# Attention of a two-layer trunk: instructions in a fixed order, weights folded in pieces with vector-engine transposes, and the values' bias as a weighted sum

## The chip, the cores and the metric

The kernel runs on one core of one Trainium2 chip. The metric is the device time of one execution in microseconds; the kernel before takes 2160.85 us, the median of three runs (2158.11 to 2163.81). All data are 32-bit floats.

## The reference

Two layers, each `x + attention(norm(x)) + ffn(norm(x))`, on x of shape (4, 512, 512).

- Layer 0's attention is a recurrence over 32 steps of 16 tokens ("TTT"): per head a small weight matrix is updated by a gradient step; the output is normalized and projected. Its feed-forward part is a gated one of width 1408.
- Layer 1's feed-forward part has four experts; every fourth token goes to the same one.
- Layer 1's attention is what the change is mainly about. Per batch, with 16 heads of 128:

```
c_kv = x @ W_DKV + b_DKV                 # 128 wide
k = c_kv @ W_UK + b_UK;  v = c_kv @ W_UV + b_UV
c_q = x @ W_DQ + b_DQ                    # 384 wide
q = c_q @ W_UQ + b_UQ
q[:, :64] = rope(q @ W_QR);  k[:, :64] = rope(k @ W_KR)   # 32 rotated, 32 zeros
out = softmax(q k^T / sqrt(128)) v @ W_O + b_O
```

## The kernel before, in words

The work lies in three stages, one after the other.

**The recurrence** (L86 to L774) steps through 32 blocks. A step is a serial chain across TensorE (PE), VectorE (DVE), ScalarE (ACT) and GpSimd (POOL). Into its gaps the program puts other work: generators yield after each piece an estimate of its PE time in us, and `fill(us)` draws pieces until the budget is spent. `GAPS`, `LAST_GAPS` and `LAST_FINISH` (L37, L38) are the budgets: three per step, and those between the parts of the last `finish`. The filler is layer 0's feed-forward part (`gate_up`, `down`), projections of the next chunk, the finishing of the chunk before (`finish`), the latents c_kv and c_q of layer 1 (`latents`, L625 on, evicted by ACT at L637 into tiles with two buffers and stored in DRAM from ACT's queue), and `value_bias` (L522). The last works out what b_UV adds to the output: softmax rows sum to one, so it is the constant row b_UV @ W_O, which goes into `bo` beside b_O. For it each of four groups of heads loads four 128 x 512 tiles of W_O (wob), multiplies them on PE with b_UV spread over 32 columns, and adds the partial rows by a product with ones.

**The experts** (L801 to L921): for each of four, gate and up products (epg, epu; PSUM tags pg, pu), SiLU on ACT, a product on DVE, and the down product (epo), which DVE adds to y (L907); POOL then adds `bo` (L908). SP, the queue of SyncE, fetches weights ahead.

**Attention** (L928 on) works in units: 4 groups of heads (hg), 4 batches (b), 4 heads of the group (h), 64 units. Before a group its weights are folded (`group_weights`, L943), so that a unit needs fewer products:

- `turned` (L933): PE turns a 128 x 512 weight by four transposes against the identity (ptw), and ACT copies the result (wt).
- `fold`: four products with W_KR or W_QR (pw) replace the second half of the key or query columns with the columns that feed the rotation.
- For values, W_UV and W_O are multiplied into vo (pvo, L970), so v is never formed.

Group 0 is folded at the start of the stage; each next one when batch 1 of the group before begins. A unit is then:

- `queries_keys` (L987): one product for keys (pk), three for queries (pq); ACT evicts 64 rows with the bias, DVE multiplies with cosine and sine (`rotate`, t_k and t_q), POOL subtracts.
- `probabilities` (L1006), four times: a product of scores (sc, four PSUM buffers), DVE's maximum (mx), ACT's exponential with the sum (prob), DVE's reciprocal, ACT's scaling.
- `softmax` and `turn` (L1017, L1041): DVE transposes 32 x 32 blocks (tt), and 16 loads on SP's queue put the blocks in place (prT).
- `context` (L1051): four products with the latent (pc), copied by ACT into ctxT.
- After the last head of a batch, `project_out` (L1063): 16 products of ctxT and vo (po), four output tiles, which DVE adds to y.

The program records keys and queries of unit i, probabilities of unit i-1 and the context of unit i-3 in one turn of its loop. The order in which an engine gets them is a scheduler's, except where `tc.keep_in_program_order` is called: then instructions marked this way stay in the order in which they were recorded. Before the change only the tail and the experts' weight loads are marked. Tiles of a pool rotate over its buffers; an instruction that writes a buffer waits for the readers of its earlier contents.

Of the kernel before, what the change touches and what calls it, by code (L numbers as in the profile page):

```python
# [12 lines left out]
F32 = mybir.dt.float32  # L13
AF = mybir.ActivationFunctionType
ALU = mybir.AluOpType
# [21 lines left out]
GAPS, LAST_GAPS = (11.0, 4.0, 8.0), (10.0, 4.0, 5.0)  # L37
LAST_FINISH = (9.0, 17.0, 5.0)  # L38
# [17 lines left out]
def trunk_kernel(ctx: ExitStack, tc: tile.TileContext, a: dict, out: bass.AP):  # L56
# [32 lines left out]
    with ExitStack() as px:  # L89
# [424 lines left out]

        ones32 = one.tile([P, P], F32, tag="ones32", name="ones32")
        nc.vector.memset(ones32, 1.0 / 32)
        buv16 = one.tile([H, D], F32, tag="buv16", name="buv16")
        nc.gpsimd.dma_start(out=buv16, in_=a["b_UV"].rearrange("(h d) -> h d", d=D))
        buv_b = one.tile([P, H, 32], F32, tag="buv_b", name="buv_b")
        nc.gpsimd.dma_start(out=bo, in_=a["b_O"].unsqueeze(0).to_broadcast([P, HS]))  # L520

        def value_bias(hg):  # L522
            if hg == 0:
                pt = psum()[:, :H]
                nc.tensor.transpose(pt, buv16, ident[:H, :H])
                nc.vector.tensor_copy(buv_b, pt.unsqueeze(2).to_broadcast([P, H, 32]))
            pb = psum()
            for h, r in enumerate(quarters):
                w = wk.tile([P, HS], F32, tag="wd", name=f"wob_{hg}_{h}", bufs=4)
                nc.sync.dma_start(out=w, in_=a["W_O"][(4 * hg + h) * D : (4 * hg + h + 1) * D, :])  # L530
                mm(pb[r], buv_b[:, 4 * hg + h, :], w)
            part = wk.tile([P, HS], F32, tag="xt", name=f"bo_part{hg}", bufs=4)
            nc.vector.tensor_copy(part, pb)
            yield 1.3
            pb = psum()
            mm(pb, ones32, part)
            nc.vector.tensor_add(bo, pb, bo)
            yield 0.86

# [84 lines left out]
        def latents(key):  # L624
# [4 lines left out]
            for m, w in enumerate(lw):  # L629
# [6 lines left out]
                for b in range(B):  # L636
                    nc.scalar.activation(  # L637
                        to[:, b], view[:, :, b // 2, :, b % 2], AF.Identity, bias=lat_b[:, m : m + 1], scale=1.0
                    )
# [6 lines left out]
        nc.gpsimd.dma_start(out=lat_b[:, :1], in_=a["b_DKV"])  # L646
        nc.gpsimd.dma_start(out=lat_b[:, 1:], in_=a["b_DQ"])


        def between(ch):  # L650
# [12 lines left out]
            extra = value_bias(ch - 1) if 1 <= ch <= NHG else iter(())  # L663
# [13 lines left out]
            yield from extra  # L677
# [120 lines left out]
        for _ in chain(work, fin, latents(NCHUNK - 1)):  # L798
            pass
# [20 lines left out]

    with ExitStack() as px:
        one = px.enter_context(tc.tile_pool(name="d_one", bufs=1, reuse_waits="tile"))
        wk = px.enter_context(tc.tile_pool(name="d_wk", bufs=2, reuse_waits="tile"))
        wg = px.enter_context(tc.tile_pool(name="d_wg", bufs=1, reuse_waits="tile"))
        psp = px.enter_context(tc.tile_pool(name="d_ps", bufs=2, space=PSUM))
        gate_w = [one.tile([P, NC, 2 * EI], F32, tag="gu1", name="gu_1")]
# [11 lines left out]
        def downs(e):  # L838
            dn = wk.tile([P, EI // P, HS], F32, tag="dn", name=f"dn_{e}")
            fetch(out=dn, in_=a["dn"][e].rearrange("(c p) o -> p c o", p=P))  # L840
            return dn
# [27 lines left out]
        for e in range(E):  # L869
# [3 lines left out]
            if e == 1:  # L873
                nc.sync.dma_start(out=wqr, in_=a["W_QR"])
                nc.sync.dma_start(out=wkr, in_=a["W_KR"])
                nc.sync.dma_start(out=buk, in_=a["b_UK"])
# [10 lines left out]
            for i in range(EI // P):  # L887
                pg = psp.tile([P, B * P], F32, tag="pg", name=f"epg_{e}_{i}")
                product(e, pg, gu, i * P)
                pu = psp.tile([P, B * P], F32, tag="pu", name=f"epu_{e}_{i}")  # L890
# [6 lines left out]
            for b in range(B):  # L897
# [10 lines left out]
                nc.gpsimd.tensor_add(y[b][:, e, :], y[b][:, e, :], bo)  # L908
            if e == 1:

                for wr, bias in ((wkr, buk), (wqr, buq)):
                    pb = psp.tile([P, 512], F32, tag="pa", name="pb")
                    nc.tensor.matmul(pb[RD:, :H], lhsT=wr, rhs=bias, start=True, stop=True)
                    nc.vector.tensor_copy(bias[RD:, :], pb[RD:, :H])
                nc.vector.tensor_scalar_mul(buq[:RD, :], buq[:RD, :], scale)
# [12 lines left out]
    with ExitStack() as px:  # L928
# [4 lines left out]
        def turned(w, nm):  # L933

            pt = ps_pj.tile([P, HPG, P], F32, tag="pj", name=f"ptw_{nm}")
            for h in range(HPG):
                nc.tensor.transpose(pt[:, h, :], w[:, h, :], ident)
            t = wk.tile([P, HPG, P], F32, tag="wt", name=f"wt_{nm}")
            nc.scalar.copy(t, pt)
            return t  # L940

        def group_weights(hg):

            c = slice(hg * HPG * D, (hg + 1) * HPG * D)

            def loaded(name, src, bufs=2):
                t = wk.tile([P, HPG, src.shape[-1] // HPG], F32, tag=name, name=f"{name}_{hg}", bufs=bufs)
                nc.sync.dma_start(out=t, in_=src.rearrange("p (h d) -> p h d", h=HPG))
                return t

            def fold(w, wr, nm):
                wt = turned(w, f"{nm}_{hg}")
# [257 lines left out]
```

## Time and profile before

| | |
|---|---|
| median of three runs | 2160.85 us |
| the profiled execution | 2162.4 us |
| its span in the profile | 2160.6 us |
| recurrence, to the first expert product | 0 to 1022.4 us |
| experts | 1022.4 to 1191.9 us |
| attention | 1191.9 to 2160.6 us |

The profile shows one execution. Rows give the source line, the engine, the operation, the output and inputs by the program's names, the shape and a count. A 32-bit product shows as two records on PE. "PEclk" is the clock granted to TensorE as a share of full speed. An "SPq" row is SyncE issuing a DMA; its duration is the issue, not the transfer. A wait row says who waited for whom, with the total in us, the number of waits and the longest. After "|", group rows give busy time, the mean duration in ns, and the idle time just before.

### The profile page before, as it was taken

The numbers are of one execution on the slowest core, as the hardware profiler recorded it, in microseconds if no ns is written. First come the engines' busy times: TensorE is split into PE (matmuls) and PEld (weight loads), VectorE is DVE, ScalarE is ACT, GpSimd is POOL, SyncE is SP. The second block draws the span as 40 slices with busy tenths as digits, with TensorE's granted clock in tenths as the row PEclk, the third lists the DMA queues.
The fourth block names the chain that finished last, engine by engine and source line by source line (L and its number), as shares of the span: only waits on it lengthen the run. The fifth ranks groups of instructions, "written<-read, shape, count | busy, mean of one in ns | idle before, by whom it ended". The sixth has DMA issues, their size and how long they took to land.

```text
span 2160.6 us, 29279 instructions
## 1 busy us (share of the span) xinstructions
PE 2068.6 (96%) x10050; PEld 1181.5 (55%) x10050; DVE 1177.5 (54%) x2384; ACT 883.3 (41%) x1805; POOL 504.9 (23%) x555
## 2 busy tenths in 40 slices
PE   8999999999999999995999899999999999999998
PEld 6776676767676767543444444444444444444444
DVE  4445656465656565631111556664666656666663
ACT  2334353434434343332000454444544545455552
POOL 4233233233333333301001211110111111111110
PEclk9999999999999999998999989999999999999999
DMA  6556364646474646526610233333233333333332
GB/s 179 153 138 190 112 193 134 180 135 175 131 197 129 173 136 192 171 75 235 226 59 25 89 92 77 74 94 75 76 77 93 75 72 78 75 75 75 95 94 76
DMA packets 286960, 259.27 MB, mean 120 GB/s; under 512 B 52956, under 2 KB 210845, under 8 KB 285789
## 3 DMA queue, kind: packets, MB, share of 16 engines
q1 hardware_dynamic: 272752, 245.96, 41.0%
q10 hardware_dynamic: 11500, 5.32, 0.9%
q0 software_dynamic: 2560, 6.13, 0.8%
q8 instruction: 81, 1.33, 0.3%
q14 instruction: 67, 0.54, 0.1%
HBM read 161.60 MB, written 29.62 MB: 89 GB/s over the span
## 4 chain that ended last, share of the span: by engine, by line
PE 75%; DVE 10%; ACT 9%; DMA 3%; issue 2%; POOL 1%; SPq 0%; ACTq 0%; DVEq 0%; POOLq 0%
PE pj L100 14%; PE pf L100 11%; PE po L1069 10%; PE pc L1054 7%; PE sc L1008 5%; PE pq L999 5%; PE pd L100 5%; ACT prob L1013 3%; PE epg L855 3%; PE epo L900 3%; PE epu L855 3%; ACT prob L1015 2%; PE pso L100 2%; PE pk L992 2%; PE pz L100 2%
## 5 line engine op out<-in xcount | busy, mean ns | idle before, releaser
L1008 PE MATMUL sc<-kT,qT 96*128 96x512 f32 x512 | 235.7, 598 | 15.1 <-ACT prob L1013 13.5
L985 POOL TENSOR_TENSOR kT<-t_k,t_k 32x512 f32<-32x512 f32 x64 | 80.7, 1261 | 717.9 <-PE pq L999 403.3
L1013 ACT ACTIVATE prob<-sc,mx 128x512 f32<-128x512 f32 x256 | 173.1, 683 | 147.1 <-DVE mx L1010 147.1
L1069 PE MATMUL po<-vo,ctxT 128*128 128x512 f32 x512 | 223.0, 593 | 1.5 <-ACT ctxT L1059 1.5
L1054 PE MATMUL pc<-prT,lv 128*128 128x512 f32 x496 | 224.0, 594 | 0.0
L1023 DVE STREAM_TRANSPOSE tt<-prob 128x512 f32<-128x512 f32 x252 | 166.6, 697 | 60.3 <-ACT prob L1015 56.7
L100 PE MATMUL pf<-xT,wg 128*128 128x256 f32 x704 | 171.8, 385 | 4.2 <-DVE hid L459 3.9
L999 PE MATMUL pq<-cq,uq 128*128 128x512 f32 x384 | 175.2, 592 | 0.0
L1015 ACT ACTIVATE prob<-prob,sm 128x512 f32<-128x512 f32 x256 | 171.7, 724 | 3.6 <-DVE sm L1014 3.6
L1008 PEld LDWEIGHTS sc<-kT,qT 96*128 96x128 f32 x512 | 96.0, 191 | 140.9 <-issue 110.6
L100 PE MATMUL pf<-xT,wu 128*128 128x256 f32 x704 | 168.0, 380 | 0.5 <-DMA wu<-in_wu 0.3
L1010 DVE TENSOR_REDUCE mx<-sc 128x1 f32<-128x512 f32 x256 | 164.4, 681 | 7.0 <-PE sc L1008 4.4
L100 PE MATMUL pd<-wd,hid 128*128 128x512 f32 x352 | 165.2, 600 | 0.2
L1069 PEld LDWEIGHTS po<-vo,ctxT 128*128 128x128 f32 x512 | 97.1, 190 | 124.1 <-issue 116.2
L1054 PEld LDWEIGHTS pc<-prT,lv 128*128 128x128 f32 x496 | 94.5, 191 | 120.0 <-issue 112.1
L100 PEld LDWEIGHTS pf<-xT,wg 128*128 128x128 f32 x704 | 131.0, 190 | 32.1 <-DVE hid L459 6.7
L100 PEld LDWEIGHTS pf<-xT,wu 128*128 128x128 f32 x704 | 133.2, 190 | 22.1 <-issue 2.6
L1079 DVE TENSOR_TENSOR y<-po,y 128x512 f32<-128x512 f32 x64 | 44.2, 691 | 152.5 <-PE po L1069 152.5
L993 ACT ACTIVATE kT<-pk,b_UK 64x512 f32<-64x512 f32 x64 | 43.7, 683 | 196.7 <-PE pk L992 196.7
L999 PEld LDWEIGHTS pq<-cq,uq 128*128 128x128 f32 x384 | 73.0, 190 | 91.8 <-issue 86.8
L459 DVE SCALAR_TENSOR_TENSOR hid<-pf,us,sg 128x256 f32<-128x256 f32 x88 | 41.5, 474 | 132.6 <-ACT sg L458 132.0
L297 POOL TENSOR_SCALAR sk<-k,m 128x256 f32<-128x256 f32 x64 | 61.3, 969 | 158.1 <-PE pz L100 158.1
(256 smaller groups left out, 3151.8 us busy)
## 6 DMA issues: line engine op xcount, KB each, us to landing
prT<-tt SPq DMA_DIRECT2D x1008, 64.0 KB, 2.0
wd<-in_wd SPq DMA_DIRECT2D x176, 256.0 KB, 3.0
wg<-in_wg SPq DMA_DIRECT2D x88, 256.0 KB, 3.5
wu<-in_wu SPq DMA_DIRECT2D x88, 256.0 KB, 3.4
rows<-rows SPq DMA_DIRECT2D x128, 66.0 KB, 2.2
kv<-rows SPq DMA_DIRECT2D x32, 264.0 KB, 4.4
gu<-in_gu SPq DMA_DIRECT2D x3, 2048.0 KB, 8.7
xt<-in_x SPq DMA_DIRECT2D x32, 128.0 KB, 3.2
```

Source lines behind the costliest of these rows:

```text
L100: nc.tensor.matmul(out, lhsT=lhsT, rhs=rhs, start=start, stop=stop, skip_group_check=True)
L855: nc.tensor.matmul(ps, lhsT=w[:, c, col : col + P], rhs=xe[:, :, c, e, :], start=(c == 0), stop=(c == NC - 1))
L900: nc.tensor.matmul(po, lhsT=inter[:, i, b * P : (b + 1) * P], rhs=dn[:, i, :], start=(i == 0), stop=(i == EI // P - 1),)
L985: nc.gpsimd.tensor_sub(t[RD:mid, :], t1[RD:mid, :], t2[RD:mid, :])
L999: nc.tensor.matmul(pq, lhsT=w["uq"][i][:, h, :], rhs=cq[:, i, b, :], start=(i == 0), stop=(i == nq - 1))
L1008: nc.tensor.matmul(ps, lhsT=qT[:KQ, i * P : (i + 1) * P], rhs=kT[:KQ, :], start=True, stop=True)
L1010: nc.vector.tensor_reduce(mx, ps, AX.X, ALU.max, negate=True)
L1013: nc.scalar.activation(pr, ps, AF.Exp, bias=mx, scale=1.0, accum_out=sm)
L1015: nc.scalar.mul(pr, pr, sm)
L1023: nc.vector.transpose(out=tt[:, :, :, i, :], in_=pr.rearrange("p (kb e j) -> p kb e j", e=2, j=K))
L1054: ins = nc.tensor.matmul(pc, lhsT=lv[:, b, k, :], rhs=prT[:, k, :], start=(k == 0), stop=(k == E - 1))
L1069: ins = nc.tensor.matmul(po[e], lhsT=ctxT[:, h, e * P : (e + 1) * P], rhs=w["vo"][:, h, :], start=(h == 0), stop=(h == HPG - 1),)
```

## The change

- **Values' bias.** `value_bias` is gone from the recurrence. Where the fold has a tile of W_O at hand, DVE adds b_UV[head] times the tile to `bo_part` (16 operations); after the last group one product with ones sums it over the partitions into `bo`. POOL adds `bo` to y in the last 16 units instead of in the experts.
- **Latents.** Odd output blocks are evicted by DVE instead of ACT; the last latents come before what is left of the filler. The budgets become `(11, 3, 8)`, `(10, 3, 7)` and `(10, 14, 7, 0, 3, 1)`.
- **Experts' pools.** Gate and up products get a PSUM pool of their own, after that of the output products; the pools' order in SBUF changes.
- **Folding by pieces.** `fold` is a generator. Per step it loads one 128 x 128-per-head weight by 16 DMAs that put 32 x 32 blocks in transposed places (32 partitions by four runs of 32 floats), DVE transposes inside the blocks (wt) a step later, and PE forms the four products (pw) another step later. PE's transposes and ACT's copies of them are gone. Group 0's fold runs among the products of experts 2 and 3; each next group's runs one step per unit, in three of four units, from batch 1 of the group before.
- **Fixed order.** All of attention's PE, DVE and ACT instructions but none of the DMAs and POOL's are marked to keep their recorded order. In the loop, exponentials of one row tile are recorded ahead of the scaling of the one before.
- **Output tiles.** `project_out` makes one tile (four products) per unit over the four units after a batch, instead of four at once.

The core of the diff:

```diff
-GAPS, LAST_GAPS = (11.0, 4.0, 8.0), (10.0, 4.0, 5.0)
-LAST_FINISH = (9.0, 17.0, 5.0)
+GAPS, LAST_GAPS = (11.0, 3.0, 8.0), (10.0, 3.0, 7.0)
+LAST_FINISH = (10.0, 14.0, 7.0, 0.0, 3.0, 1.0)
...
-            extra = value_bias(ch - 1) if 1 <= ch <= NHG else iter(())
...
+                    if m % 2:
+                        nc.vector.tensor_scalar(to[:, b], part_b, lat_b[:, m : m + 1], None, ALU.add)
+                    else:
+                        nc.scalar.activation(to[:, b], part_b, AF.Identity, bias=lat_b[:, m : m + 1], scale=1.0)
...
-        for _ in chain(work, fin, latents(NCHUNK - 1)):
+        for _ in chain(latents(NCHUNK - 1), work):
...
+    def fold(w, hg, wk, psum, bufs, pin=lambda ins: ins):
...
+        for i in range(n + 2):
+            if 0 <= i - 2 < n - 1:
+                wt, wr, to = turned.pop(i - 2), wkr if i == 2 else wqr, w[ups[i - 2]]
+                pw = psum(f"pw_{hg}_{i}").rearrange("p (h d) -> p h d", h=HPG)[:, :, :RD]
+                for h in range(HPG):
+                    pin(nc.tensor.matmul(pw[:, h, :], lhsT=wt[:, h, :], rhs=wr, start=True, stop=True))
+                pin(nc.scalar.copy(to[:, :, RD:], pw))
+            if 0 <= i - 1 < n:
+                t = turned[i - 1] = wk.tile([P, HPG, P], F32, tag="wt", name=f"wt_{hg}_{i - 1}", bufs=bufs)
+                pin(
+                    nc.vector.transpose(
+                        out=t.rearrange("p h c -> p (h c)"), in_=raws.pop(i - 1).rearrange("p h c -> p (h c)")
+                    )
+                )
+            if i < n:
+                raw = raws[i] = wk.tile([P, HPG, P], F32, tag="raw", name=f"raw_{hg}_{i}", bufs=bufs)
+                view = srcs[i].rearrange("(cq r) (h dq d) -> dq r h cq d", r=32, h=HPG, dq=4)
+                for dq, r in enumerate(quarters):
+                    for h in range(HPG):
+                        nc.sync.dma_start(
+                            out=raw[r, h].rearrange("r (cq d) -> r cq d", cq=4), in_=view[dq, :, h]
+                        )
+            if i >= n:
+                output_rows(i - n)
+            yield
...
+            pv = psum(f"pvo_{hg}_{h}")
+            pin(nc.tensor.matmul(pv, lhsT=wt[:, h, :], rhs=ows[h], start=True, stop=True))
+            pin(nc.scalar.copy(w["vo"][:, h, :], pv))
...
+                pin(nc.vector.scalar_tensor_tensor(bo_part, ows[h], buv[:, hh : hh + 1], bo_part, ALU.mult, ALU.add))
...
+            pin(nc.tensor.matmul(pb, lhsT=ones, rhs=bo_part, start=True, stop=True))
...
+        wd = px.enter_context(tc.tile_pool(name="d_wd", bufs=2, reuse_waits="tile"))
+        wg = px.enter_context(tc.tile_pool(name="d_wg", bufs=1, reuse_waits="tile"))
         wk = px.enter_context(tc.tile_pool(name="d_wk", bufs=2, reuse_waits="tile"))
-        wg = px.enter_context(tc.tile_pool(name="d_wg", bufs=1, reuse_waits="tile"))
         psp = px.enter_context(tc.tile_pool(name="d_ps", bufs=2, space=PSUM))
+        ps_gu = px.enter_context(tc.tile_pool(name="d_psgu", bufs=2, space=PSUM))
...
-                nc.gpsimd.tensor_add(y[b][:, e, :], y[b][:, e, :], bo)
...
+        def pin(ins):
+            tc.keep_in_program_order(ins)
+            return ins
...
                 if h == 0:
                     if b == 1 and hg + 1 < NHG:
-                        ws[hg + 1] = group_weights(hg + 1)
+                        ws[hg + 1] = group_tiles((lat, wk)[(hg + 1) % 2], hg + 1)
+                        folds = fold(
+                            ws[hg + 1], hg + 1, wk, lambda nm: ps_pj.tile([P, 512], F32, tag="pj", name=nm), 2, pin
+                        )
...
+            for _ in range(1 if i < nu - 1 else 2):
+                if outs:
+                    outs.pop(0)()
             if i >= 3:
                 hg, b, h = units[i - 3]
                 context(probs.pop(i - 3), b, cs[hg, b], h, f"{i - 3}")
                 if h == HPG - 1:
-                    project_out(hg, b, ws[hg], cs[hg, b], range(HPG), {})
...
+                    outs += [
+                        (lambda hg=hg, b=b, e=e: project_out(hg, b, e, ws[hg], cs[hg, b], range(HPG), {}))
+                        for e in range(E)
+                    ]
+            if i % HPG != 0:
+                next(folds, None)
+            k = i - (nu - HPG * B)
+            if 0 <= k < HPG * B:
+                b, e = divmod(k, HPG)
+                nc.gpsimd.tensor_add(y[b][:, e, :], y[b][:, e, :], bo)
```

## The prediction

> **What bounds the kernel now.** I read the page first, then PE's waits in two stretches, the groups of PE by line and shape, the stages as windows, and last SyncE's part of the timeline.
>
> ```profile
> span 2160.6 us, 29279 instructions
> PE 2068.6 (96%) x10050; PEld 1181.5 (55%) x10050; DVE 1177.5 (54%) x2384; ACT 883.3 (41%) x1805; POOL 504.9 (23%) x555
> PEclk9999999999999999998999989999999999999999
> ```
>
> TensorE is busy for 96% of the span: a change pays by removing PE work, PE waits, or time at the reduced clock, which shows in two slices. Two neighbouring rows of PE's timeline give the price of a product, and two others that of four transposes:
>
> ```profile
> 1505.84 3.60 PE L1054 MATMUL pc<-prT,lv 128*128 128x512 f32 x8
> 1509.27 1.02 PE L992 MATMUL pk<-ckv,uk 128*128 128x512 f32 x2
> ...
> 1486.42 0.60 PE L937 MATMUL ptw_uk<-ident,uk 128*128 128x128 f32 x4
> 1486.86 1.88 PE L1008 MATMUL sc<-kT,qT 96*128 96x512 f32 x4
> ```
>
> A product is two records. Eight records take 3.43 us from start to start, so a product is 0.858 us; four transposes are 0.44. A unit (a head of a batch) has 16 products, 13.7 us; 64 units are 879 of the 968.7 us from the first fold transpose (1191.9) to the end. The rest is folding, waits and clock. PE's waits in attention, then from 955 to 1030:
>
> ```profile
> PE sc L1008 <- ACT prob L1013: 13.5, 13, 4.0
> PE pw_uq L955 <- ACT wt_uq L939: 8.4, 10, 1.2
> PE pvo L970 <- ACT wt_uv L939: 2.8, 4, 0.7
> PE sc L1008 <- POOL qT L985: 1.7, 2, 1.4
> ...
> PE pj L100 <- DVE pn_sq L543: 11.7, 1, 11.7
> PE epg L855 <- ACT lat L637: 6.7, 1, 6.7
> ```
>
> The last column is the longest wait. Twelve of the 13 waits for the exponentials are thus short, about one per batch of four heads. The stages show where the clock is missing (the seventh figure, after POOL's busy time):
>
> ```profile
> core 0: us, PE busy (x) PEld busy (x) DVE busy (x) ACT busy (x) POOL busy (x), PEclk, DMA share, GB/s
> 960.00:1022.40 62.40, 36.06 (x116) 21.51 (x115) 16.39 (x20) 18.18 (x57) 10.60 (x16) 0.87 0.55 184
> 1191.90:1209.60 17.70, 13.29 (x62) 9.07 (x62) 0.69 (x1) 6.17 (x12) 1.26 (x1) 0.81 0.37 135
> 1209.60:1291.00 81.40, 72.44 (x189) 34.60 (x188) 49.58 (x90) 45.61 (x92) 16.93 (x14) 0.90 0.32 84
> 1560.00:2115.00 555.00, 545.31 (x1304) 242.08 (x1303) 362.29 (x662) 279.01 (x599) 97.02 (x77) 1.00 0.33 81
> ```
>
> In the steady part PE is busy 545 of 555 us at full clock; little is left there. The losses are at the two joints.
>
> **The change part by part.** The sum is made against the profiled execution, 2162.4 us (span 2160.6); that is 1.5 above the median 2160.85.
>
> *Values' bias.* It leaves the recurrence:
>
> ```profile
> L100 PE MATMUL pj<-wob,buv_b 128*32 128x512 f32 x32 | 13.0, 619 | 0.0
> L100 PE MATMUL pj<-bo_part,ones 128*128 128x512 f32 x8 | 4.2, 605 | 0.0
> ```
>
> With one transpose (0.2) that is 17.4 us of PE in a stage where PE is busy 96 to 100% from 100 to 960. Added: one product in attention (0.86) and one transpose (0.2). The weighted sums are 16 vector operations of 128x512, about 0.7 us each by the y additions, on a vector engine busy 65% of attention. The sixteen bias additions on POOL (1.27 each) move into the last 16 units, where POOL works 2.5 us per unit. Balance: **-16.3**. The changed gaps (23 to 22 per step) only keep the total of planned filler near the smaller work, so that latents are left to fill the end.
>
> *End of the recurrence.* From 955 to 1022.4 PE waits 26.3 us, and loses some 6 by the clock (0.87 in that window, and it stays so until 1040). The 11.7 comes from the last normalization: ScalarE stands from 981 to 989.7 behind a latent tile whose store has not landed. The 6.7 is the first expert product, waiting for a PSUM buffer which the last latent evictions free. The change moves half of those evictions to DVE, leaves about 59 us of PE work behind the last recurrent product (50 before, clock losses included), and gives the gate products buffers that the latents don't use. The chain of the last normalization, by its rows, is about 41 us to the last eviction before the final latents, so it fits under that work. I keep 8 us of loss: two hand-overs of 1 to 2 us in that chain and some clock. **-24**. Both sides: nothing recovered but the 6.7, or all 32.
>
> *Folding.* 80 transposes go (4 x 5 x 4), 20 x 0.45 = **-9.0**. The waits that followed each (8.4 + 2.8 + 0.7 + 0.8) go too, because the turned tile comes from DVE a step earlier: **-12.7**. The products stay; group 0's 7 us move under the experts, where they are the same PE time. DVE gains 20 block transposes at 0.70 (the tt row's mean); ACT loses 20 copies.
>
> *Clock.* 0.81 of 17.7 us and 0.90 of 81.4 us lose 3.4 + 8.1 = 11.5 us, and a little more in the products that straddle it. The pages' rule ("TensorE: Matmul & The Clock Gate", What's actually happening) is that a whole idle window of about 3.4 us is what halves the clock. Here it was half with no idle gap over 1.2 us in the fold before it, only small products. By the rule I would save the single loss after the 4.0 us wait, some 5 us; by the rows, all. Since the small products at the joint are spread among large ones, I take the rows: **-12**.
>
> *Fixed order.* In the new order PE does per unit: keys and queries of unit i, four scores of i-1, one output tile, context of i-3. Scores then need exponentials of the unit before, a whole unit earlier, so the twelve short waits go. At the start there is no output work: PE asks for 6.9 us per unit twice, then 10.3 four times, while one unit on DVE takes 4 x (0.70 + 0.68 + 0.16) + 4 x 0.75 = 9.2 plus hand-overs to ACT, some 11.8. Four score buffers and double tiles let PE run about 10 ahead; 71 - 55 - 10 = 6 us stay. Of 15.2 us of score waits: **-9**. Later a unit's vector chain, with the output addition, is 11.5 to 12.7 us of 13.7, and fits.
>
> *What it adds: SyncE's queue.* This is the step that decides.
>
> ```profile
> 1500.22 10.24 SPq L1046 DMA_DIRECT2D prT<-tt  x16
> ...
> L1046 SPq DMA_DIRECT2D prT<-tt x1008: 585/599/1982, 1227.7 to 2137.0; - x168
> L879 SPq DMA_DIRECT2D trig_k<-in_trig x4: 596/1021/2371, 1033.9 to 1041.0; - x4
> ```
>
> Sixteen turns of a unit already hold SP for 10.2 of 13.7 us. Each fold step adds 16 loads in front of the next unit's turns, on the same queue: 80 per group, 32 partitions by 4 runs of 128 bytes. No row has that form. The floor is a plain weight load, 0.33 to 0.45 us (uk, uv); the ceiling trig_k, 64-byte runs, 0.6 to 2.4, median 1.0. I take prT's 0.64 from start to start, of the same 32 by 4 runs. A fold unit then costs SP 20.5 us against 14.6 on PE. Waiting behind it: the vector transpose of a piece, pinned before the next unit's rotations, so a late piece stops DVE, and with it qT and the exponentials. Steps come in pairs of consecutive units; by the second the queue lags 11 us, the piece lands 13 to 18 us after DVE asked, and PE tolerates about 10 (the buffers again). I count 4 us for group 1 (its first 30 loads go out under the experts) and 6 for each of the other two: **+16**. At 0.5 us or less the lag stays under 8 and the cost is 0. In the expert stage a step there is 16 x 0.64 + 2 to land + 0.7, 13 us, against two products of 6.9 and the output products between: no wait by my walk.
>
> The Trainium skill speaks against these loads: "DMA: Bandwidth & Descriptors", Rules for kernel authors, says to coalesce, since under 64 KB one pays mostly overhead; these are 16 KB. Its section Issuing engines are not separate DMA queues calls the issue time usually small beside the transfer. By that page the price would fall on the 16 shared engines, busy 33% here, and cost nothing; by the prT row it falls on the queue (10.2 us of issue against 2.0 to land). I follow the row.
>
> *Sum:* -16.3 - 24 - 9.0 - 12.7 - 12 - 9 + 16 = -67. 2162.4 - 67 = 2095; less the 1.5: **2093 us**.
>
> **The rivals.** *SP is cheap* (0.15): at 0.35 to 0.45 us the pieces never come late, the 16 goes, and the end of the recurrence may close fully (8): 2068 to 2078. For it: every load from DRAM by 128 partitions. Against: prT.
>
> *The fixed order has its own waits* (0.17): DVE's order can't change, so where ACT and DVE hand over slower than the rows' durations, a unit grows past 13.7 us. The 1 us of slack in the 12.7 is thin: 0.7 us more per unit over 60 units, 42 us, gives 2135. For it: DVE idled 72.6 us behind kT in the kernel before. Against: those waits shrink when DVE is late.
>
> *Slower* (0.11): the loads of pieces at 1 us or more, as trig_k's. SP then needs 26 us per fold unit; the lag reaches 27 to 38 us, the pair of steps costs PE about 30 us in two groups and 23 in the first, 83 in all against 83 gained. The point is 1.05 us per load; at 1.2 it gives about 2185. For it: short runs. Against: trig_k stood behind the two bias loads of 4-byte packets just before it (b_UK alone 1.8 us), and its last, clean one took 0.6.
>
> *It doesn't do what it says:* the turns stay fixed only where instructions are pinned, and they are on PE, DVE and ACT; I give this no chance of its own.
>
> **How the numbers follow.** My case 0.57, 2080 to 2110 around 2093; the rivals 0.15, 0.17 and 0.11. The range takes in the cheap queue and most of the slow hand-overs: 2068 to 2138. A difference within 0.3% (6.5 us) can't be told from none. Faster 0.85, same 0.05, slower 0.10.
>
> **What would show it.** No wob or ptw rows; the recurrence's end and expert start about 40 us earlier, with no wait of 6.7 before the first gate product; PE's clock 1.0 from the first unit; score waits under 7 us in all. On SP, 80 loads of pieces per group: their start-to-start time decides between the cases, and a wait of DVE's transpose (wt) for the piece should show in fold units, with PE's waits just after. Wrong would be: steady waits of sc or pc in every unit (hand-overs), or PE waiting for pw or wt in the experts.

## The result, and the profile after

The changed kernel takes 2127.05 us, the median of four runs (2124.80 to 2127.84); the kernel before, beside it, 2160.94 (2158.11 to 2163.81). The ratio is 0.9841, 95% interval 0.9824 to 0.9858: 34 us faster, where 67 were forecast. The time lies inside the range and nearer to its upper end; the sign is as forecast, the size is half.

The head of the page after, to be laid beside the three lines shown of before:

```profile
span 2125.1 us, 29355 instructions
PE 2041.5 (96%) x9932; PEld 1169.6 (55%) x9932; DVE 1199.9 (56%) x2452; ACT 860.5 (40%) x1733; POOL 504.4 (24%) x555
PEclk9999999999999999999999999999999999999999
```

118 records and 27 us of TensorE's busy time are gone, but its share is still 96%. The forty slices hide where it stands; the stages show it. I cut both traces at the same three events:

| us | before | after | difference | forecast |
|---|---|---|---|---|
| start to first gate product (epg) | 1022.4 | 1008.5 | -13.9 | -40 |
| experts, and what precedes attention | 169.5 | 185.0 | +15.5 | +7 |
| attention, with its folding | 968.7 | 931.6 | -37.1 | -34 |
| sum | 2160.6 | 2125.1 | -35.5 | -67 |

("Attention" starts at the first fold transpose before and at the first key product after, since group 0 is folded among the experts now.) So the attention is as forecast; 26 of the missing 32 us are lost in the recurrence and behind it, and 8 in the experts. TensorE's waits of after, from the start to 1060 us (who waited for whom, us in total, count, longest):

```profile
PE wacc L100 <- DVE g_bd L378: 11.5, 3, 9.3
PE pf L100 <- DVE hid L459: 7.1, 5, 3.1
PE epu L906 <- DVE inter L951: 7.0, 1, 7.0
PE pj L100 <- DVE lat L613: 5.1, 2, 4.0
PE pj L100 <- ACT lat L615: 4.9, 3, 3.5
PE pj L100 <- ACT pn_sq L524: 4.4, 2, 2.9
```

The wait of 6.7 for the PSUM buffer of the first gate product and the 11.7 for the last normalization are gone, as forecast. Three others stand in their place: 9.3 us in the first step of the recurrence's last chunk (step 28), 10 us for latents at its end, 7.0 in expert 0. The windows of after, of the last chunk, the joint between recurrence and experts, and attention's start and first units (seventh figure: granted clock):

```profile
840.00:930.00 90.00, 79.45 (x666) 51.52 (x665) 53.96 (x121) 25.00 (x52) 25.70 (x28) 0.94 0.46 135
930.00:1008.50 78.50, 64.98 (x177) 34.44 (x176) 24.03 (x52) 16.76 (x49) 10.76 (x17) 0.89 0.49 154
1192.50:1210.00 17.50, 16.29 (x38) 7.05 (x38) 11.07 (x20) 8.85 (x17) 5.05 (x4) 1.00 0.22 36
1210.00:1291.00 81.00, 76.40 (x179) 33.40 (x178) 64.88 (x120) 50.65 (x107) 17.65 (x14) 0.98 0.40 93
```

At attention's start the clock is 1.00 and 0.98 where it was 0.81 and 0.90. At the joint it is still 0.89, and the last chunk, at 1.00 before, now has 0.94. (Below, "half-clock time" is the sum of the stretches that a trace records at a granted clock of 0.50.) TensorE's waits in attention:

```profile
PE pq L1028 <- ACT ctxT L1108: 7.3, 3, 3.7
PE pvo L854 <- DMA ow<-in_W_O: 3.7, 3, 2.1
PE pc L1106 <- DVE t_q L1003: 3.2, 1, 3.2
PE sc L1038 <- ACT prob L1043: 1.4, 2, 1.1
```

Scores wait 1.4 us for exponentials instead of 13.5, and no row has a turned weight. What is new are one wait of 3.2 us for pc in the first units, and three of pq and three of pvo, one pair for each group folded during attention.

**Where pq's wait comes from.** It names a copy on ACT, but the chain is longer. SyncE's rows, then DVE's, then ScalarE's and TensorE's, around the last pieces of group 1:

```profile
1305.90 10.76 SPq L1098 DMA_DIRECT2D prT<-tt  x16
1316.70 7.72 SPq L845 DMA_DIRECT2D raw<-in_W_UQ  x16
1324.53 10.24 SPq L1098 DMA_DIRECT2D prT<-tt  x16
1334.82 7.72 SPq L845 DMA_DIRECT2D raw<-in_W_UV  x16
```

```profile
1326.20 0.71 DVE L835 STREAM_TRANSPOSE wt<-raw 128x512 f32<-128x512 f32 x1 [9.89 <-DMA raw<-in_W_UQ]
...
1330.08 1.29 DVE L1040 TENSOR_REDUCE mx<-sc 128x1 f32<-128x512 f32 x2
```

```profile
1330.81 0.69 ACT L1043 ACTIVATE prob<-sc,mx 128x512 f32<-128x512 f32 x1 [9.00 <-DVE mx L1040]
...
1336.12 0.57 ACT L1108 COPY ctxT<-pc 128x512 f32<-128x512 f32 x1
```

```profile
1336.74 3.94 PE L1028 MATMUL pq<-cq,uq 128*128 128x512 f32 x5 [3.66 <-ACT ctxT L1108]
```

The 16 loads of a piece are issued from 1316.7 to 1324.4, behind the 16 turns of a unit, and DVE stands 9.89 us for them. Behind the transpose in DVE's fixed order are the rotations and maxima of the unit, so ACT stands 9.00; behind ACT's exponentials is the copy that frees the buffer that pq needs. TensorE still has work for 6.2 of those microseconds and waits 3.66. The other two groups agree: DVE stands 8.40 and 7.68 us, and pq waits 2.17 and 1.45, again 6.2 less. The waits of pvo are for tiles of W_O, whose loads stand behind turns on the same queue. This is the path that the prediction described, with one number off: a load takes 7.83 / 16 = 0.49 us from start to start, not 0.64.

### The profile page after: what moved, and what is told of

It is laid out like the page before. It is cut to its first block, busy times and chain, and to the rows that moved or that the text cites. A ratio compares the mean times of both kernels' runs of the same rounds, so it can differ in the third digit from the quotient of the medians.

```text
span 2125.1 us, 29355 instructions
## 1 busy us (share of the span) xinstructions
PE 2041.5 (96%) x9932; PEld 1169.6 (55%) x9932; DVE 1199.9 (56%) x2452; ACT 860.5 (40%) x1733; POOL 504.4 (24%) x555
## 2 busy tenths in 40 slices
DMA packets 336496, 257.19 MB, mean 121 GB/s; under 512 B 107099, under 2 KB 264988, under 8 KB 335324
## 4 chain that ended last, share of the span: by engine, by line
PE 78%; DVE 6%; SPq 6%; DMA 4%; ACT 3%; issue 2%; POOL 1%; ACTq 0%; DVEq 0%; POOLq 0%
PE pj L100 14%; PE pf L100 11%; PE po L1119 9%; PE pc L1106 8%; PE sc L1038 8%; PE pq L1028 7%; PE pd L100 5%; SPq L1098 4%; PE epo L957 3%; PE epu L906 2%; PE pso L100 2%; PE pk L1020 2%; PE epg L906 2%; PE pz L100 2%; SPq L845 1%
## 5 line engine op out<-in xcount | busy, mean ns | idle before, releaser
L1038 PE MATMUL sc<-kT,qT 96*128 96x512 f32 x512 | 230.9, 593 | 1.7 <-ACT prob L1043 1.4
L1119 PE MATMUL po<-vo,ctxT 128*128 128x512 f32 x512 | 230.0, 592 | 0.7 <-ACT ctxT L1108 0.7
L1067 DVE STREAM_TRANSPOSE tt<-prob 128x512 f32<-128x512 f32 x252 | 173.0, 706 | 56.2 <-ACT prob L1048 48.5
L1048 ACT ACTIVATE prob<-prob,sm 128x512 f32<-128x512 f32 x256 | 176.4, 713 | 0.0
L1003 DVE SCALAR_TENSOR_TENSOR t_k<-pk,b_UK,trig_k 32x512 f32<-32x512 f32 x64 | 47.9, 748 | 90.4 <-ACT kT L1021 89.8
L100 PEld LDWEIGHTS pd<-wd,hid 128*128 128x128 f32 x352 | 63.8, 190 | 61.8 <-issue 48.6
```

The lines of the kernel that those rows point to most:

```text
L100: nc.tensor.matmul(out, lhsT=lhsT, rhs=rhs, start=start, stop=stop, skip_group_check=True)
L1038: pin(nc.tensor.matmul(ps, lhsT=qT[:KQ, i * P : (i + 1) * P], rhs=kT[:KQ, :], start=True, stop=True))
L1048: pin(nc.scalar.mul(pr, pr, sm))
L1067: nc.vector.transpose(out=tt[:, :, :, i, :], in_=pr.rearrange("p (kb e j) -> p kb e j", e=2, j=K))
L1119: nc.tensor.matmul(po[e], lhsT=ctxT[:, h, e * P : (e + 1) * P], rhs=w["vo"][:, h, :], start=(h == 0), stop=(h == HPG - 1),)
```

## The experiments

Twelve kernels ran. "Changed" means the changed kernel, 2127.05 us. Each was timed beside the kernel before (medians 2161.45, 2162.41, 2162.99 and 2162.67 in the four sets); the ratio is to that. Differences between two kernels are of medians, and the kernel before alone moves by 2 us from set to set, so 1 or 2 us say nothing; where stages are compared, they are of the profiled executions.

### The pieces on SyncE's queue

**e_plain.** One load per folding step instead of 16.

```diff
-                for dq, r in enumerate(quarters):
-                    for h in range(HPG):
-                        nc.sync.dma_start(
-                            out=raw[r, h].rearrange("r (cq d) -> r cq d", cq=4), in_=view[dq, :, h]
-                        )
+                nc.sync.dma_start(out=raw, in_=srcs[i].rearrange("p (h d) -> p h d", h=HPG))
```

> Changed kernel with each fold step's 16 piece loads replaced by one plain load of the same weight (the blocks then are not moved to their transposed places, so the folded weights differ from the reference; all other instructions stay). Theory (late pieces on the sync queue): DVE's waits for a piece (7 to 10 us each) vanish, the waits of PE for queries and for output rows in the fold units (7.3 and 3.7 us) vanish, attention shrinks by 9 to 11 us, time about 2117. Rival (the waits come from PSUM buffers, which the folded products take from the queries): attention within 3 us of before.

Measured: 2111.22 us, ratio 0.9761 [0.9742, 0.9780], 16 less than changed. The waits of pq and pvo have no row any more, nor has a wait of DVE for a piece; attention is 916.4 us instead of 931.6. That is more than the 9 to 11 expected: besides 11.0 us of waits, half-clock time in attention falls from 10.2 to 5.1 us. (One wait of 3.6 us for pc stays in the first units, where the changed kernel has 3.2.) The pieces cost what the prediction gave them, 16 us.

**e_twice.** Every piece loaded twice, into the same place.

```diff
+                for again in range(2):
+                    for dq, r in enumerate(quarters):
...
```

> Changed kernel with every piece loaded twice, 32 loads per fold step. A piece load took 0.43 us of issue in the changed kernel, some 0.48 from start to start, so a fold unit holds the sync queue 10.3 + 15.4 = 25.7 us against 14.6 on PE: this is the case that the prediction's slower rival describes (1 us per piece). By that reckoning PE loses about 30 us in each of two groups and 23 in the first: about 70 us more than the changed kernel, 2200. Rival (the queue catches up in the units without a step, PE's tolerance is larger than 10 us): under 35 us more.

Measured: 2236.43 us, ratio 1.0345 [1.0316, 1.0375], 109 more than changed and slower than before: by more than either theory gave. TensorE's waits of e_twice from 1180 us on:

```profile
PE pc L1107 <- DMA prT<-tt: 22.9, 4, 7.2
PE pw L830 <- DVE t_k L1010: 22.6, 3, 8.3
PE pq L1029 <- ACT ctxT L1109: 18.8, 7, 4.4
PE pk L1021 <- DVE t_k L1010: 18.1, 6, 4.7
```

DVE now stands 164 us for pieces (120.7 and 43.7 in two rows), and with 32 x 0.49 + 10.3 = 26 us of queue per folding unit even the turns come late (pc for prT). That is the load on the queue at which the prediction put its slower rival; against e_plain the price is 125 us, where the rival had 83.

**e_spread.** The same loads, one folding step every second unit. (The products of W_UV and W_O move with their steps, to units 0 and 2 of the next group, and the additions of `bo` come four units later.)

```diff
-            if i % HPG != 0:
+            if i % (HPG * B) in (0, 2, 4, 6, 8, 10, 12, 14, 15):
                 next(folds, None)
...
```

> The changed kernel with the five loading steps of each later fold two units apart (units 4, 6, 8, 10 and 12 of the group before) and the products of values and W_O in units 0 and 2 of the next group, the additions of bo four units later; the same loads on the same queue, the same work. Theory (a piece is late because its loads stand behind the 10.2 us of turns of the same unit, and DVE asks for it one unit later): with two units between, the queue has 27 us for 27.8 minus what stands in the other units, no wait of wt for raw over 1 us, no waits of pq for ctxT and of pvo for ow (7.3 and 3.7 us in the changed kernel), and the clock dips in attention go: 2127 - 12 = 2115. Rival (the loads cost by their number, through the DMA engines): the waits stay, 2127 within 4.

Measured: 2112.80 us, ratio 0.9773 [0.9745, 0.9800], 14 less than changed. All pq and pvo waits are gone, as in e_plain, and DVE waits for no piece, with all 240 loads still there. So neither the number of loads nor their 16 KB costs anything that can be told from e_plain's time; their spacing does. In the rows above, DVE's last block transpose ahead of the late piece ended at 1301.1; the turns that need it started at 1305.9, 4.8 us late, because another step's loads had held the queue from 1287.0 to 1295.1. Then come 10.8 us of turns, 7.8 of loads and 1.8 to the start of DVE's transpose, 25 us together, where DVE asks after 15. With two units between steps the 4.8 goes, and DVE asks after 29.

### The fixed order

**e_nopin.** Attention's instructions are left to the scheduler; only those behind the last unit stay marked.

```diff
+        fixed = []
+
         def pin(ins):
-            tc.keep_in_program_order(ins)
+            if fixed:
+                tc.keep_in_program_order(ins)
             return ins
...
+        fixed.append(1)
```

> The changed kernel with attention's instructions no longer kept in their recorded order (except those behind the last unit, as before). Theory of the prediction: the fixed order is worth about 9 us, so short waits of scores for exponentials come back, 2127 + 9 = 2136. Rival: the order of the scheduler is as good, since the two differ only in waits of 1 us, and a late piece no longer stops the rotations behind it: 2127 or less, down to 2116.

Measured: 2162.94 us, ratio 1.0000 [0.9983, 1.0016], 36 more than changed: without the fixed order the whole gain is gone. Both theories were too small. TensorE's waits of e_nopin from 1191 us on, and its window where after had 71.4 of 76 us busy at 0.98:

```profile
PE sc L1041 <- POOL qT L1016: 23.0, 17, 3.9
PE pw L830 <- DVE wt L835: 8.6, 3, 3.0
PE sc L1041 <- ACT prob L1046: 4.5, 1, 4.5
```

```profile
1215.00:1291.00 76.00, 62.43 (x116) 26.06 (x116) 44.58 (x85) 36.05 (x76) 12.58 (x10) 0.82 0.32 76
```

It is not the exponentials that come late but the rotated queries, which POOL forms from DVE's products. The rows of TensorE and POOL show why, first in e_nopin, then TensorE's in the changed kernel:

```profile
1245.25 2.74 PE L1031 MATMUL pq<-cq,uq 128*128 128x512 f32 x6
1247.82 1.02 PE L1041 MATMUL sc<-kT,qT 96*128 96x512 f32 x2
1250.56 1.25 POOL L1016 TENSOR_TENSOR qT<-t_q,t_q 32x512 f32<-32x512 f32 x1 [1.14 <-DVE t_q L1012]
1251.87 7.09 PE L1041 MATMUL sc<-kT,qT 96*128 96x512 f32 x8 [3.02 <-POOL qT L1016]
```

```profile
1240.06 2.74 PE L1028 MATMUL pq<-cq,uq 128*128 128x512 f32 x6
1242.64 3.60 PE L1038 MATMUL sc<-kT,qT 96*128 96x512 f32 x8
```

In e_nopin the scheduler puts a unit's scores one product behind its own queries. Between them ScalarE's copy (1248.1), DVE's two products (from 1248.9) and POOL's subtraction follow each other at once; that takes 4 us, and TensorE has 0.9 us of work for it. In the fixed order the scores behind the queries are those of the unit before: they start at 1242.64, before ScalarE copies these queries at 1242.90. The waits in attention grow by 20 us (17.5 to 37.6). They are short, but from 1218 to 1276 each comes with a stretch at half clock; half-clock time in attention goes from 10 to 44 us, which at half speed is another 17. Together that is 37 of the 38 us by which attention is longer.

### The joint and the experts

**e_lat3.** Three buffers instead of two for the tile that the latents share with other stores.

```diff
-                st = wk.tile([P, 512], F32, tag="xs", name=f"lat_{ks[0]}_{m}")
+                st = wk.tile([P, 512], F32, tag="xs", name=f"lat_{ks[0]}_{m}", bufs=3)
...
```

> Changed kernel with three instead of two buffers for the tile into which latents are evicted. Theory (the end of the recurrence is held by evictions that wait for stores, each about 8 us): the waits of the last latents for stores (11.4 on ACT, 5.4 and 4.3 on DVE) shrink, PE's waits from 930 us to the first expert product go from 13.6 to 6 to 9, and the time drops by 4 to 9 us to about 2120. Rival (the chain of the last normalization is itself too long for the work behind it): PE waits as long, now for the normalization, and less than 2 us are gained.

Measured: 2118.14 us, ratio 0.9799 [0.9777, 0.9820], 9 less than changed. The joint, from the last recurrent product to the first gate product, takes 71.1 us instead of 79.9, and its waits 8.9 instead of 13.5. With evictions on two engines both stood for the stores of latents two tiles back: in the changed kernel 12.1 us on DVE and 14.2 on ACT; with three buffers none on DVE and 6.4 on ACT.

**e_trig.** The scaled sine, a single DVE operation, comes one expert later, and is marked to keep its order together with the experts' products of gate and up.

```diff
-                nc.vector.tensor_scalar_mul(trig_q[RD:, :], trig_k[RD:, :], scale)
             if e == 2:
+                tc.keep_in_program_order(nc.vector.tensor_scalar_mul(trig_q[RD:, :], trig_k[RD:, :], scale))
...
```

> Changed kernel, but the query's scaled table (trig_q from trig_k) is multiplied on the vector engine after expert 2 instead of among the products of expert 0. Theory (in-order vector queue): in the changed kernel that one multiplication waits 22 us for its table and holds the gate-up product of expert 0, so PE loses 7.0 us and some 3.4 more at half clock; here the wait is gone, the expert stage shrinks from 184 to about 174 us, and the time is about 2117 (10 less than 2127). Rival (the wait would only be replaced by another at the same joint, as for the SiLU or an output-row load): less than 3 us gained.

Measured: 2117.69 us, ratio 0.9794 [0.9770, 0.9818], 9 less than changed. The wait in expert 0 is gone, with the 6.8 us of half clock behind it, and the experts take 175.7 us instead of 185.0. DVE's row of that operation, before and after the change, says why:

```profile
1043.54 0.42 DVE L916 TENSOR_SCALAR trig_q<-trig_k 64x512 f32<-64x512 f32 x1 [11.05 <-DMA trig_k<-in_trig]
```

```profile
1038.50 0.42 DVE L977 TENSOR_SCALAR trig_q<-trig_k 64x512 f32<-64x512 f32 x1 [22.21 <-DMA trig_k<-in_trig]
```

The program records trig_q behind expert 1; the scheduler put it among expert 0's products in both kernels, and DVE stood there for a table that SyncE had not yet fetched. Behind it in DVE's order is a product of gate and up, which frees the PSUM buffer of a later up product. Before the change trig_q came 21 us after the first gate product, and no TensorE wait followed. In the changed kernel the experts start 13.9 us earlier, but SyncE issues the table's first load only 5.7 us earlier (1028.2 instead of 1033.9), so trig_q comes 30 us after the first gate product, and TensorE waits 7.0. The new pool is not the cause: gate and up had two buffers each before, too. What holds SyncE back there was not tried.

### The recurrence: the budgets

**e_budget.** The changed kernel with the budgets of before.

```diff
-GAPS, LAST_GAPS = (11.0, 3.0, 8.0), (10.0, 3.0, 7.0)
-LAST_FINISH = (10.0, 14.0, 7.0, 0.0, 3.0, 1.0)
+GAPS, LAST_GAPS = (11.0, 4.0, 8.0), (10.0, 4.0, 5.0)
+LAST_FINISH = (9.0, 17.0, 5.0, 0.0, 0.0, 0.0)
```

> The changed kernel with the budgets of the kernel before: (11, 4, 8) and (10, 4, 5) per step and (9, 17, 5, 0, 0, 0) for the last normalization. Theory: the hole of 9.3 us at 841 comes from the smaller budgets, which leave filler short in a step of the last chunk while DVE works on reciprocals; with 4 instead of 3 it goes, and the recurrence ends 5 to 10 us earlier against the work done in it, but less filler is left behind its end, so the joint gets some of it back: 2122. Rival: the hole is the order of the filler (reciprocals of DVE before the step's own operations), not its amount: it stays, 2127 within 3.

Measured: 2152.70 us, ratio 0.9958 [0.9944, 0.9973]: 26 more than changed. The hole at 841 goes, but others open at the same place of every chunk: 3.15 us for hid and 1.90 for pn_sq, 116 us apart from 277 to 742 us, the same two as in e_nobias below, which also has the old budgets without the values' bias. Both theories fell, and with them the prediction's remark that the budgets only match the amount of filler.

**e_nobias.** The kernel before, without the values' bias in the recurrence.

```diff
-            extra = value_bias(ch - 1) if 1 <= ch <= NHG else iter(())
+            extra = iter(())
```

> The kernel before without the generator of the values' bias (the term from b_UV is left out of the output), its budgets and everything else as before. Theory of the prediction: 17.4 us of TensorE's work leave a stage that TensorE fills, so 2161 - 17 = 2144. Rival, after the run with the old budgets (first expert product at 1034 against 1022 before, although the same work was out): the old budgets, with less filler, draw pieces whose inputs are not ready (hid, pn_sq), and the gain is eaten by waits at the same place of every chunk and by the clock: 2161 to 2173.

Measured: 2187.92 us, ratio 1.0112 [1.0095, 1.0129]: 25 us *more* with 17 us less to do. TensorE's waits of e_nobias to 1050 us; in before the same two rows had 7.9 and 3.9 us up to 930, and then the 11.7:

```profile
PE pj L100 <- DVE pn_sq L543: 22.9, 9, 6.7
PE pf L100 <- DVE hid L459: 18.2, 7, 3.2
```

One wait of 3.15 us for hid and one of 1.90 for pn_sq stand in five chunks in a row, 116 us apart, each of the longer ones with 3.4 us of half clock. To the first gate product TensorE's waits grow by 22 us against before, and half-clock time goes from 26 to 59 us. With less filler and the same budgets, the pieces come earlier in the chunk, and those that need DVE or ACT meet it when the step needs it too; this last is a reading of the rows around one such wait, not tried by itself.

**e_small.** The kernel before, with the changed kernel's first two budgets.

```diff
-GAPS, LAST_GAPS = (11.0, 4.0, 8.0), (10.0, 4.0, 5.0)
+GAPS, LAST_GAPS = (11.0, 3.0, 8.0), (10.0, 3.0, 7.0)
```

> The kernel before with the changed kernel's first two budgets, (11, 3, 8) and (10, 3, 7), the values' bias still in the recurrence. If the budgets only have to match the amount of filler, as the prediction put it: TensorE's work is the same, less of it lies before the end of the recurrence and more behind, where the waits of 26 us stand: 2161 - 10 = 2151, with the recurrence's last product 15 to 25 us earlier. Rival: too small a budget opens gaps in every step that were filled: 2161 or more.

Measured: 2201.93 us, ratio 1.0174 [1.0156, 1.0191]: 39 more than before. Each half of the change makes the kernel slower, by 25 and by 39, and both together (with the other edits) bring the experts' start forward by 13.9. TensorE's waits of e_small to 1060 us:

```profile
PE wacc L100 <- DVE g_bd L378: 15.6, 3, 8.8
PE wacc L100 <- ACT g_bd L378: 10.5, 1, 10.5
```

Nearly all of it is three holes, at 651, 774 and 893 us, of the kind that the changed kernel has once. DVE's rows of the changed kernel at its hole (841 to 851):

```profile
834.49 3.35 DVE L531 RECIPROCAL pn_rs<-pn_rs 128x512 f32<-128x512 f32 x1 [2.46 <-ACT pn_rs L530]
...
839.38 3.35 DVE L531 RECIPROCAL pn_rs<-pn_rs 128x512 f32<-128x512 f32 x1 [0.81 <-ACT pn_rs L530]
842.65 0.11 DVE L350 TENSOR_TENSOR rl<-r,kv 128x16 f32<-128x16 f32 x1
...
845.12 2.56 DVE L370 TENSOR_TENSOR xh<-xh,s 128x256 f32<-128x256 f32 x1
...
849.70 0.87 DVE L378 COPY g_bd<-grad 32x256 f32<-32x256 f32 x2
```

Two reciprocals of the finishing of the chunk before, 3.35 us each, stand ahead of the step's own chain to g_bd, which TensorE then waits for with its filler behind the waiting product. One operation of the chain, at 845.12, took 2.56 us besides (see the last section).

**e_small2.** e_small with the reciprocals drawn two pieces later and kept behind the gradient copies of each chunk's first step.

```diff
+                if be < 2 and n % CH == 0:
+                    tc.keep_in_program_order(ins)
...
+                if ch < NCHUNK - 1:
+                    tc.keep_in_program_order(ins)
...
-                if i == NI - 3:
+                if i == NI - 3 + 2:
```

> The kernel of e_small (before, with the smaller budgets; 2202 us), with the two reciprocals of a normalization drawn two pieces of filler later and kept behind the gradient copies of each chunk's first step, so that on DVE they no longer stand ahead of the gradients of steps 20, 24 and 28 but behind those of 21, 25 and 29. Theory (budgets act through where the 3.35 us reciprocals fall on DVE): the three waits of TensorE for the gradient, 26 us, and about 10 us of half clock behind them go: 2202 - 30 = 2172, within 10. Rival (the small budgets leave too little filler in every step): waits of the same size open at other steps, 2202 within 6.

Measured: 2185.75 us, ratio 1.0112 [1.0084, 1.0141], 16 less than e_small, between theory and rival. The three holes are gone: the waits for g_bd are 3.4 us in all, none over 1.1, and half-clock time before the last recurrent product falls from 41 to 24 us. But the waits for pn_sq, on DVE and ACT, grow from 11 to 18. So the place of the reciprocals explains the holes and 16 of the 39 us that the small budgets cost; the other 23 are not explained.

### Together

**e_best** joins e_trig, e_lat3 and e_spread.

> The scaled sine kept in its place behind the experts' products (as in e_trig), three buffers for the latents (as in e_lat3), and the folds' steps two units apart (as in e_spread), together. If the three are independent: 2127 - 9.5 - 9 - 12 = 2097. If the earlier expert start only moves waits to a later place: 2105 to 2110.

Measured: 2096.83 us, ratio 0.9704 [0.9676, 0.9732]: 30.2 us below changed, where the three alone gave 9.4, 8.9 and 14.3, together 32.5. Within the noise they are independent; that 2097 was met so closely comes of e_spread having been reckoned at 12.

**e_best3** adds to it the marks on the two reciprocals of the last-but-one finishing and the gradient copies of step 28 (the first two edits of e_small2, for that chunk alone).

> The three changes of e_best, and the last-but-one normalization's two reciprocals on DVE kept behind the copies of the gradient of step 28 (with which they competed at 834 to 843). If the wait of 9.3 us of TensorE for that gradient and the 10 us of half clock behind it go and nothing takes their place: 2097 - 9 - 5 = 2083. If the reciprocals only stop a later step: 2097 within 3.

Measured: 2084.79 us (2084.13 to 2085.42), ratio 0.9638 [0.9624, 0.9652], the fastest kernel here: 78 us below before. Its waits and clock, to be laid beside those of after:

```profile
span 2082.7 us, 29373 instructions
PE 2030.1 (97%) x9932; PEld 1164.4 (56%) x9932; DVE 1198.1 (58%) x2452; ACT 865.9 (42%) x1735; POOL 505.3 (24%) x555
...
PEclk9999999999999999999999999999999999999999
```

```profile
PE pf L100 <- DVE hid L461: 6.9, 4, 3.1
PE pj L100 <- ACT lat L619: 5.3, 3, 3.9
PE pj L100 <- ACT pn_sq L526: 4.4, 2, 2.9
...
PE wacc L100 <- DVE g_bd L378: 2.4, 2, 1.6
```

The wait for g_bd is 2.4 in all instead of 11.5, and up to the last recurrent product TensorE waits 31 us, where it waited 32 before the change and 41 after; the first gate product is at 991.0, 31 us ahead of before, where the prediction wanted 40.

## Why the prediction was right and wrong

The number lies in the range, but not for a reason that the range was drawn for: the pieces were not cheap, and the rival nearest in number, waits of the fixed order itself (2135), did not come. The range was wide enough to take in losses in the recurrence, at the joint and in the experts that no rival named.

**Right: attention.** Forecast -34, measured -37. Transposes -12.6 (forecast -9.0; four took 0.63 us on average, not 0.44). Waits from the first fold transpose on 29.4 to 17.5, -11.9, where folding waits, order and pieces together were put at -5.7. Half-clock time went from 24 to 10 us, so about -7 where -12 was forecast; e_spread, in which only the 6.8 us of half clock at the start are left, shows that the other dips came from the late pieces. That is some 31.5 together; the rest, 5.6, fits group 0's products, which are in the experts now (forecast 7). Between the rule and the rows that the prediction weighed, neither holds alone: in after, half clock follows waits of 3.19, 3.66 and 2.10 us (1224, 1337, 1842 us), and none follows one of 2.17 (1568).

**Right with a wrong working: the pieces.** The +16 is what e_plain gives, through the chain that was described: the queue has not caught up when the next step's loads come, and DVE waits. But a load cost 0.49 us, and by the prediction's rule (at 0.5 or less "the cost is 0") there would have been none. The 0.64 was taken from the turns, "of the same 32 by 4 runs"; the pieces have as many runs, but each is a quarter as long. The rule rested on "PE tolerates about 10": the piece above was 9.89 us late, and TensorE waited 3.66 of them, so it tolerates about 6. A price too high and a tolerance too wide cancelled: luck. The same tolerance made the slower rival too mild: at 26 us of queue per unit it had 83 us, e_twice shows 125. The rule of the Trainium skill ("DMA: Bandwidth & Descriptors", Rules for kernel authors) that one should coalesce is worth 16 us here, though not by an overhead in the shared engines: with the same small loads, e_spread has no such cost. What its section Issuing engines are not separate DMA queues says, that issue time is usually small beside the transfer, agrees for a single piece (0.43 us of issue, 1.8 to land); it is the sum on one queue, 18 us of issue in a unit of 14.6, that makes the wait.

**Wrong: the values' bias.** "-16.3", with the remark that the changed gaps "only keep the total of planned filler near the smaller work". The recurrence is full of TensorE work, but it isn't a sum: e_nobias takes the work out and loses 25 us, e_small takes only the gaps and loses 39. A budget decides which piece of filler meets which step, and a finishing that puts two reciprocals ahead of a gradient costs 9 us and some clock (e_best3: 12 us). With that one meeting put right, the recurrence waits no longer than before the change, with the values' bias out of it.

**Wrong in size: the joint.** "-24" with "8 us of loss" kept. 13.5 us of waits and 17 us of half clock (some 8 us of loss, an estimate from its length) stayed. The step that failed was that the chain "fits under that work": it reckoned evictions by their own rows and left out that a tile has two buffers and that its store must land. That was visible: the 8.7 us for which ACT stood behind a latent's store in before were read as the cause of the 11.7, and taken as removed by a second evicting engine, which doubles the rate at which buffers are asked for. e_lat3 gives 9 back; the rest stays open.

**Wrong: the experts.** The prediction has "no wait by my walk" of a folding step there. The walk followed the pieces, and those made no wait of TensorE. It did not ask whether the other inputs of the stage come as much earlier as its start does. The table for trig_q did not, and the margin that hid this one DVE operation before the change was gone: 9.4 us by e_trig.

**Wrong in size: the fixed order.** Waits of scores fell as forecast, but the 9 us were reckoned against the kernel before and from exponentials alone. In the new sequence of work the fixed order carries 36 us, because it keeps a unit's worth of products between queries and their scores; about half of it lies in the clock.

## What to carry to other kernels

A stage that one engine fills is not a sum of its work: where filler is drawn by budgets, taking work out moves every later piece, so look which long operation of another engine lands ahead of the step's own chain, and keep that pair in order by hand. When an in-order queue has as much to do as its stage has time, a burst of loads that is not yet worked off makes the next one late, so space the bursts out before counting descriptors. When a stage starts earlier, ask which of its inputs do not. When a second engine is given half of the evictions, count the buffers and the landing of their stores anew.

## What the runs showed of the hardware that was not expected

- Sixteen 16 KB loads, each 32 partitions by four runs of 128 bytes, hold SyncE 0.49 us each, less than the 0.64 of the 64 KB turns, whose 32 by 4 runs are 512 bytes long: here the number of runs alone did not set the price. The packets under 512 bytes doubled (52956 in the page of before, 107099 after) with no cost of their own in e_spread.
- A vector operation of 128x256 took 2.56 us (845.12 to 847.68, above) instead of the 0.42 that it has in the same step of e_best3, while GpSimd's addition of zb ran:

```profile
844.90 2.50 POOL L537 TENSOR_TENSOR zb<-zb,q 128x1024 f32<-128x1024 f32 x1 [12.96 <-ACT zb L534]
```

  The same operation has 2.57 us in e_small. The Trainium skill ("SBUF — State Buffer", Terms) has these two engines take turns at one pair of ports, the loser blocked for the whole instruction; the common end, within 0.3 us, agrees, but no run separated the two, so this is a reading.
- Short waits that come back keep the clock low: in e_nopin four waits of TensorE, 4.5, 2.2, 3.0 and 3.9 us long and 15 to 18 us apart, each came with 6.8 us at half clock, and over 76 us, 62.4 of them busy, the granted clock was 0.82.
